# Two chained cross-attentions in f32: scores computed once and kept in SBUF, with their maxima sent round through DRAM

## The chip, the core and the metric

The kernel runs on one core of a Trainium2 chip. Its engines are named as the profile names them: PE is TensorE (matrix products), DVE is VectorE, ACT is ScalarE, POOL is GpSimd, SP is SyncE, which here issues every DMA. SBUF is the on-chip memory, PSUM the memory that TensorE writes into. The metric is device time in microseconds (us) of one execution.

## The reference

There are 4 batches, 512 queries of width C = 320, and 1024 context rows of width 512; 20 heads of 16 columns each. Two layers run one after the other, and the second takes the first one's result as its queries.

```python
# layer 0: text keys are context rows 0..1019, image ("ip") keys the last 4
q = heads(x @ W_q)
probs_t = softmax(q @ heads(text @ W_k).T * 0.25)
text_out = probs_t @ heads(text @ W_v)
qsem = l2norm(probs_t @ text)                  # 512 wide, per head and query
fused = q @ heads(ip @ W_k_ip).T * 0.25 + 0.5 * qsem @ l2norm(ip).T
ip_out = softmax(fused) * spatial_mask @ heads(ip @ W_v_ip)
x1 = (text_out + ip_out) @ W_out + b_out + x

# layer 1: text keys are context rows 0..76, ip keys the other 947
q = heads(x1 @ Wq.T)
out = softmax(q @ k_text.T * 0.25) @ v_text + softmax(q @ k_ip.T * 0.25) @ v_ip
return out @ Wo.T + bo + x1
```

The costly part is `probs_t @ text`: for each head it multiplies 512 x 1020 probabilities by a 1020 x 512 context, of which only the row norms and four inner products are needed.

## The kernel before

**Units.** A batch is cut in two halves of 256 queries (SH), a half in ten pairs of heads: 4 x 2 x 10 = 80 pair groups, counted by gi. One group has two units (class Head, one for each head). A unit multiplies exponentials of the scores by the context through a Strassen-like scheme: seven products instead of eight, each of four matmuls with 128 stationary columns, in four parts: part0 (products with context blocks 11 and 21, each also carrying value columns), part1 (t1, t2), part2 (22, t3), part3 (t4). Between them stand small sums: POOL forms s2 of two blocks of exponentials (L754), adds it to one block and subtracts it from another (L771, L774); ACT copies p and u out of PSUM (L769, L786); DVE copies p of block t1 (L782, "p5" in the code), adds c from PSUM (L762), and ACT squares and sums (L758). The products write to three PSUM banks. Value columns are loaded as narrow "windows" beside the context blocks by DMAs (L715).

**Scores, twice.** Each pair's scores are computed two times. max_fill (L437) puts 128 queries stationary and streams 512 keys; DVE takes the maximum over the keys from PSUM, negated (L663 in layer 0; L505 and L506 in layer 1). The negated maxima are transposed (pt_nm) and added to three extra rows of the queries (qa; L470 through subtract_max L462 in layer 0, L517 in layer 1). exp_fill (L448) computes the scores again with 19 rows, 16 of the head and three that carry the maxima, keys stationary and queries streaming, so that PSUM holds scores less the maximum; ACT takes the exponential directly from PSUM (L459), and for layer 0 POOL subtracts one query block from the other (L675). Each fill has one of two PSUM buffers (ps_sc).

**Order.** A list written out by hand sets it. Between the parts of a unit stand stops. stop_a (two per unit) puts a max_fill of group gi+2 and an exp_fill of group gi+1; stop_b (two per unit) takes a step of layer 1 (layer1_half L485, step L586: one max_fill of the next four heads, one exp_fill of these, and now and then the products with the values, do_pv); both also take one piece of other work from the queues: early and late (the end of a turn: softmax of the four ip scores, W_out, transposes, the queries of layer 1), proj (keys and values of the next batch). stop_c takes further steps of layer 1 near the end. The prologue computes all keys and values of batch 0. After the last group what is left of layer 1, a half batch, runs by itself. Engines take their instructions in order, and DMAs wait on SP's queue in order.

All matrix products go through one helper, mm (L74), and transposes through tr (L77), so the profile shows them under these lines; they are told apart by the tiles that they write: b (unit), mx and ex (scores), pv (layer 1's values), pt_ (others).

Of the kernel before, what the change touches and what calls it, by code (L numbers as in the profile page):

```python
# [20 lines left out]
P = 128  # L21
# [3 lines left out]
NIP = 4  # L25
# [8 lines left out]
SH = S // 2  # L34
NP = H // 2
QT = 256


R_TXT, R_IP, R_ALL, KR = 16, 17, 18, 19
# [7 lines left out]
NEVER = -1e30  # L47
ATTN_SCALE = 0.25
# [5 lines left out]
def xattn_pair(ctx_stack: ExitStack, tc: tile.TileContext, a: dict, out: bass.AP):  # L54
# [8 lines left out]
    ep = pool("ep", 8)  # L63
    st2 = pool("st2", 2)
# [13 lines left out]

    idle = [True]
# [22 lines left out]
    kq = [[cst.tile([P, T], F32, name=f"kq{l}_{i}") for i in range(1 + l)] for l in range(2)]  # L102
    qq = [[cst.tile([P, SH], F32, name=f"qq{l}_{i}") for i in range(1 + l)] for l in range(2)]
    nmz = [[cst.tile([P, 2, P], F32, name=f"nmz{l}_{i}") for i in range(1 + l)] for l in range(2)]
# [6 lines left out]
    last = cst.tile([P, 2], F32, name="last")  # L111
    wq = [cst.tile([P, NC, C], F32, name=f"wq{i}") for i in range(2)]
# [9 lines left out]
    def load_x(b, sh, pl, tag):  # L122
        t = pl.tile([P, 2, C], F32, tag=tag, name=f"{tag}_{b}_{sh}")
        nc.sync.dma_start(t, a["x"][b, sh * SH : (sh + 1) * SH, :].rearrange("(t p) c -> p t c", p=P))
        return t
# [3 lines left out]
    def load_w(b, *names):  # L129
# [11 lines left out]
        if names == ("L0_xattn_W_v",):  # L141
# [4 lines left out]

    load_chunks(wq[0], "L0_xattn_W_q")
    nc.scalar.dma_start(bo[0], a["L0_xattn_b_out"].partition_broadcast(P))


    rows0 = st3.tile([2, T], F32, tag="e1", name="rows0")
    nc.gpsimd.memset(rows0, 1.0)
    nc.gpsimd.affine_select(out=rows0[:, 0:NTXT0], in_=rows0[:, 0:NTXT0], compare_op=ALU.not_equal, fill=0.0, base=-1,
                            pattern=[[0, NTXT0]], channel_multiplier=1)

    rows = st3.tile([3, T], F32, tag="e1", name="rows")
    nc.gpsimd.memset(rows, 1.0)
    nc.gpsimd.affine_select(out=rows[:, 0:NTXT1], in_=rows[:, 0:NTXT1], compare_op=ALU.not_equal, fill=0.0, base=-1,
                            pattern=[[0, NTXT1]], channel_multiplier=1)
    nc.gpsimd.affine_select(out=rows[:, NTXT1:T], in_=rows[:, NTXT1:T], compare_op=ALU.not_equal, fill=0.0, base=0,  # L160
                            pattern=[[0, T - NTXT1]], channel_multiplier=1)
    for l in range(2):
        for i in range(1 + l):
            nc.vector.memset(qq[l][i], 0.0)
            nc.vector.memset(nmz[l][i], 0.0)
            for r in range(4):
                if l:
                    nc.scalar.dma_start(kq[l][i][32 * r + R_TXT : 32 * r + KR, :], rows)
                else:
                    nc.scalar.dma_start(kq[l][i][32 * r + R_ALL : 32 * r + KR, :], rows0[0:1, :])  # L170
                    nc.scalar.dma_start(kq[l][i][32 * r + R_IP : 32 * r + R_ALL, :], rows0[1:2, :])
                    nc.scalar.dma_start(kq[l][i][32 * r + R_TXT : 32 * r + R_IP, :], rows0[1:2, :])
    nc.vector.memset(nmz[0][0].rearrange("p j (r n) -> p (j r) n", r=4)[:, :, R_IP], NEVER)
# [3 lines left out]
                            pattern=[[0, 2]], channel_multiplier=-1)  # L177
    for n in ("21", "t4"):
        nc.gpsimd.memset(xv[n], 0.0)
# [38 lines left out]
    def transposed_half(src, name, tag):  # L218

        t = big.tile([P, NC, SH], F32, tag=tag, name=name)  # L220

        def front():
            pt = tp(f"pt_{name}_a")
            for c in range(2):
                for j in range(2):
                    tr(pt[:, c * SH + j * P : c * SH + (j + 1) * P], src[:, j, c * P : (c + 1) * P], ident)
            evac(t[:, 0:2, :].rearrange("p c s -> p (c s)"), pt)

        def back():
            pt = tp(f"pt_{name}_b")  # L230
            for j in range(2):
                tr(pt[:64, j * P : (j + 1) * P], src[:, j, 2 * P : C], ident)
            evac(t[:64, 2, :], pt[:64, 0:SH])

        return t, [front, back]

    def queries(t, w, dst, name, tag):

        o = (st2 if tag == "kst" else big).tile([P, NC, SH], F32, tag=tag, name=f"qs_{name}")

        def front():
            pt = tp(f"pt_{name}_a")
            for c in range(2):
                for i, (_, n) in enumerate(CK):
                    mm(pt[:, c * SH : (c + 1) * SH], w[:n, i, c * P : (c + 1) * P], t[:n, i, :], i == 0, i == NC - 1)
            nc.vector.tensor_scalar(o[:, 0:2, :].rearrange("p c s -> p (c s)"), pt, ATTN_SCALE, None, ALU.mult)

        def back():
            pt = tp(f"pt_{name}_b")
            for i, (_, n) in enumerate(CK):  # L250
                mm(pt[:64, 0:SH], w[:n, i, 2 * P : C], t[:n, i, :], i == 0, i == NC - 1)
            nc.vector.tensor_scalar(o[:64, 2, :], pt[:64, 0:SH], ATTN_SCALE, None, ALU.mult)
            nc.sync.dma_start(dst[0 : 2 * P, :].rearrange("(c p) s -> p c s", p=P), o[:, 0:2, :])
            nc.sync.dma_start(dst[2 * P : C, :], o[:64, 2, :])

        return [front, back]

    def projections(b):
# [5 lines left out]
        z.qd = [[dr.tile([C, SH], F32, tag=f"q{l}_{sh}", name=f"qd{l}_{b}_{sh}") for sh in range(2)] for l in range(2)]  # L264
# [4 lines left out]
        def quarter(n):  # L269
# [4 lines left out]
            def buffer(tag, shape):  # L274

                return (big if b else ep).tile(shape, F32, tag=tag if b else "e0", name=f"{tag}_{b}_{n}")
# [118 lines left out]
            if n == 0:  # L395
                v1[0:1] = [lambda: values1_first(0), lambda: values1_first(1)]
            return [[lambda: turn(0), lambda: (turn(1), sums())], [lambda: keys(0)], [lambda: keys(1)], [last_keys],
                    [lambda: values0(0), lambda: values0(1)], v1, [values_ip] if n == 3 else []]

        quarters = [quarter(n) for n in range(4)]  # L400

        for kinds in quarters if b else zip(*quarters):
            for kind in kinds:
                steps += kind
        for sh in range(2):
            hold = {}

            def first(sh=sh, hold=hold):
                t, hold["x"] = transposed_half(load_x(b, sh, big, "xin"), f"xT0_{b}_{sh}", "raw")
                hold["q"] = queries(t, wq[0], z.qd[0][sh], f"q0_{b}_{sh}", "kst")  # L410
                hold["x"][0]()

            steps += [first, lambda hold=hold: hold["x"][1](), lambda hold=hold: hold["q"][0](),
                      lambda hold=hold: hold["q"][1]()]
        return z, steps


    def pair(p):
        return p // 2, 2 * (p % 2)

    def place(l, turn, p):


        g, r0 = pair(p)
        return buffer(l, turn, g), r0

    def buffer(l, turn, g):
        return (turn * HG + g) % 2 if l else 0

    def load_pair(l, z, turn, g, i):  # L430
        k = buffer(l, turn, g)
        for r in range(2 * i, 2 * i + 2):
            c = 64 * g + 16 * r
# [580 lines left out]
```

## Time and profile before

| | us |
|---|---|
| median of 3 runs | 3852.46 (3849.34 to 3853.75) |
| profiled execution | 3851.3 |
| its span | 3849.6 |
| TensorE busy | 3710.9 (96%) |
| VectorE busy | 1622.4 (42%) |
| ScalarE busy | 1195.9 (31%) |
| GpSimd busy | 1033.4 (27%) |
| first and last unit product | 196.1, 3624.8 |

The busy times are sums over the instructions of an engine, in the one profiled execution; its span is the time from the first to the last recorded event, 1.7 us less than the time of that execution. In the views a row of the timeline has the start, the duration, the engine, the line of the code, the operation, the tile written and the tiles read, the shape, and in brackets how long the engine had idled and what released it. A row of the windows has, for a stretch of time, the busy time of PE, weight loads, DVE, ACT and POOL, then the granted clock of TensorE as a fraction of full speed, the share of the DMA engines, and GB/s.

### The profile page before, as it was taken

Reading aid. Unit: us, or ns where it says so; the run is one execution under the profiler, and the core shown is the slowest. Engines: PE = TensorE matmul, PEld = TensorE weight load, DVE = VectorE, ACT = ScalarE, POOL = GpSimd, SP = SyncE. Lnnn points to the kernel's source line nnn. Section 1 sums busy time; section 2 is a strip of 40 time slices with the busy share of each in tenths; the row PEclk is TensorE's granted clock in tenths of the full one; section 3 lists DMA queues with packets and bytes.
Section 4 is the critical chain, followed back from the end, with each engine's and each line's share of the span. In section 5 each row is a group of like instructions: output and inputs, shape, how many; then the busy total and the mean of one; then the engine's idle time right before and its main releaser. Section 6 shows DMA issues by size and latency. Waiting matters only on the chain.

```text
span 3849.6 us, 57354 instructions
## 1 busy us (share of the span) xinstructions
PE 3710.9 (96%) x21972; PEld 2633.4 (68%) x21972; DVE 1622.4 (42%) x3089; ACT 1195.9 (31%) x2424; POOL 1033.4 (27%) x1376
## 2 busy tenths in 40 slices
PE   5899999999999999999999999999999999999887
PEld 4577777677776777767776777767776676766533
DVE  1222234444434445344543545334544445355343
ACT  0122223233322333323332333323333333233222
POOL 1032233233322222223322222223332332322100
PEclk9899999999999999999999999999999999999955
DMA  6424411111232231211223232211211111111100
GB/s 178 121 67 109 108 41 17 18 28 23 59 74 64 66 89 37 53 37 28 67 52 76 62 74 48 53 34 28 61 22 31 29 22 26 30 21 25 24 19 13
DMA packets 541488, 196.11 MB, mean 51 GB/s; under 512 B 428056, under 2 KB 530936, under 8 KB 541216
## 3 DMA queue, kind: packets, MB, share of 16 engines
q1 hardware_dynamic: 540608, 192.10, 22.0%
q8 instruction: 175, 2.87, 0.3%
q14 instruction: 97, 0.79, 0.1%
q10 hardware_dynamic: 608, 0.35, 0.0%
HBM read 149.39 MB, written 40.16 MB: 49 GB/s over the span
## 4 chain that ended last, share of the span: by engine, by line
PE 91%; DVE 4%; DMA 3%; issue 1%; SPq 0%; ACT 0%; POOL 0%; POOLq 0%; DVEq 0%; ACTq 0%
PE b L74 53%; PE mx L74 11%; PE ex L74 9%; PE pv L74 5%; PE pt_k L74 4%; PE pt_v L74 4%; PE pt_y L74 2%; PE pt_q_a L74 1%; DVE den L550 1%; DVE m L506 1%; PE pt_nm L77 1%; DMA v1d<-v 1%; DMA raw<-in_ctx_dram 1%; PE pt_q_b L74 1%; DVE den L547 0%
## 5 line engine op out<-in xcount | busy, mean ns | idle before, releaser
L459 ACT ACTIVATE e<-ex 128x1024 f32<-128x1024 f32 x640 | 654.7, 1023 | 658.6 <-PE ex L74 655.6
L74 PE MATMUL ex<-qa,kq 19*128 19x256 f32 x5120 | 759.0, 417 | 10.1 <-DVE qa L517 7.3
L74 PE MATMUL mx<-kq,qq 16*128 16x512 f32 x2560 | 732.1, 673 | 28.1 <-DVE m L506 20.2
L74 PE MATMUL b<-xv_t,e 128*128 128x277 f32 x2560 | 674.2, 406 | 6.2 <-DVE c L762 6.0
L74 PE MATMUL b<-xv,e 128*128 128x277 f32 x2560 | 639.7, 402 | 0.5 <-DVE qa L470 0.5
L74 PEld LDWEIGHTS b<-xv_t,e 128*128 128x128 f32 x2560 | 471.5, 190 | 169.5 <-issue 54.0
L74 PEld LDWEIGHTS b<-xv,e 128*128 128x128 f32 x2560 | 473.8, 190 | 151.4 <-issue 44.8
L74 PEld LDWEIGHTS ex<-qa,kq 19*128 19x128 f32 x5120 | 454.9, 192 | 79.7 <-issue 16.7
L663 DVE TENSOR_REDUCE m<-mx 128x2 f32<-128x1024 f32 x320 | 390.0, 1219 | 222.5 <-PE ex L74 215.7
L758 ACT ACTIVATE junk<-c 128x256 f32<-128x256 f32 x480 | 200.2, 417 | 879.1 <-DVE c L762 879.0
L754 POOL TENSOR_TENSOR s<-e,e 128x256 f32<-128x256 f32 x320 | 228.6, 725 | 796.7 <-ACT e L459 648.3
L506 DVE TENSOR_REDUCE m<-mx 128x2 f32<-128x870 f32 (+1 forms) x320 | 364.4, 1139 | 170.1 <-PE ex L74 152.5
L675 POOL TENSOR_TENSOR e<-e 128x512 f32<-128x512 f32 x160 | 204.6, 1279 | 785.4 <-ACT e L459 776.7
L762 DVE TENSOR_TENSOR c<-b,p 128x256 f32<-128x256 f32 x320 | 134.1, 419 | 611.6 <-PE b L74 568.6
L74 PEld LDWEIGHTS mx<-kq,qq 16*128 16x128 f32 x2560 | 195.8, 191 | 246.6 <-issue 185.8
L74 PE MATMUL b<-xs,e 128*128 128x256 f32 x1280 | 318.6, 392 | 3.6 <-DVE p L782 3.6
L74 PE MATMUL b<-xs_t,e 128*128 128x256 f32 x1280 | 319.4, 392 | 1.4 <-POOL e L771 1.4
L771 POOL TENSOR_TENSOR e<-e,s 128x256 f32<-128x256 f32 x320 | 232.4, 728 | 325.9 <-PE b L74 325.9
L74 PE MATMUL b<-xs_t,s 128*128 128x256 f32 x1280 | 307.5, 383 | 0.0
L74 PEld LDWEIGHTS b<-xs,e 128*128 128x128 f32 x1280 | 233.5, 191 | 81.9 <-issue 41.6
L74 PEld LDWEIGHTS b<-xs_t,e 128*128 128x128 f32 x1280 | 229.9, 189 | 79.6 <-issue 26.2
L74 PEld LDWEIGHTS b<-xs_t,s 128*128 128x128 f32 x1280 | 241.7, 191 | 47.4 <-issue 15.6
(190 smaller groups left out, 2907.8 us busy)
## 6 DMA issues: line engine op xcount, KB each, us to landing
kq<-kd SPq DMA_DIRECT2D x320, 64.0 KB
v1q<-v1d SPq DMA_DIRECT2D x40, 373.5 KB
xv<-v0d SPq DMA_DIRECT2D x320, 42.0 KB
xv_t<-v0d SPq DMA_DIRECT2D x320, 42.0 KB
L_xattn_W_k<-in_L_xattn_W_k_dram SPq DMA_DIRECT2D x13, 640.0 KB
L_xattn_W_v<-in_L_xattn_W_v_dram SPq DMA_DIRECT2D x13, 640.0 KB
raw<-in_ctx_dram SPq DMA_DIRECT2D x32, 256.0 KB
td<-sums SPq DMA_DIRECT2D x64, 128.0 KB
```

What stands on the lines that cost most here:

```text
L74: tc.keep_in_program_order(nc.tensor.matmul(out, lhsT=lhsT, rhs=rhs, start=start, stop=stop, skip_group_check=on))
L77: tc.keep_in_program_order(nc.tensor.transpose(out, in_, ident))
L459: nc.scalar.activation(e.rearrange("p i j s -> p (i j s)"), ps.rearrange("p i n -> p (i n)"), AF.Exp)
L506: nc.vector.tensor_reduce(m[:, half, :], ps[:, :, 0 if half else NTXT1 : 512], AX.X, ALU.max, negate=True)
L550: nc.vector.reciprocal(d[:, k * SH : (k + 1) * SH], d[:, k * SH : (k + 1) * SH])
L663: nc.vector.tensor_reduce(ms[gi][:, j, half, :], ps[:, :, 0:n], AX.X, ALU.max, negate=True)
L675: nc.gpsimd.tensor_tensor(e[:, :, :, P:SH], e[:, :, :, P:SH], e[:, :, :, 0:P], ALU.subtract)
L754: nc.gpsimd.tensor_tensor(self.s2[:, 2 * k : 2 * k + 2, :], self.e("21", k), self.e("22", k), ALU.add)
L758: nc.scalar.activation(junk, x, AF.Square, accum_out=self.w["ss"][:, j, self.h, k : k + 1])
L762: nc.vector.tensor_tensor(c, x, y, ALU.add)
L771: nc.gpsimd.tensor_tensor(self.e("11", k), self.e("11", k), self.s2[:, 2 * k : 2 * k + 2, :], ALU.add)
```

## The change

Scores are computed once. A turn is now 128 queries (TURNS, 16 of them), and a group four heads of one turn: 16 x 5 = 80 groups, again of two units (class Unit, two heads each; the two row blocks of the scheme are now two heads, before they were two query tiles of one head).

fill computes half of the keys for all four heads, keys stationary, 128 queries streaming, in both ps_sc buffers; ACT copies the raw scores to SBUF (L443), and DVE takes the maximum over the four key tiles, from PSUM, for each key row and query (L444). Two fills make a group's scores. A combine joins the two halves (L617, L620; L483 in layer 1). max0 (layer 0) and do_max (layer 1) transpose these maxima (4 or 8 transposes), DVE reduces them over what were rows (L633; L495, L496), and spread (L448) transposes the result in 32 x 32 blocks (L451) and writes it to DRAM by four DMAs (L454). A DMA reads it back to all 128 partitions as bc (L637; three of them, L501 to L503, in layer 1). Then bc is added to the raw scores in SBUF, by DVE (L642, L644; L510, and half of L511 and L514) and POOL (L645; the other half of L511 and L514), and ACT takes the exponential in place (L648, L516). POOL's subtraction follows (L650).

The adds wait in a queue of their own, ew: two are taken at the end of a stop, later(1, ...) says how many stops after the maxima. The stop after part k of a group's eight parts: k = 0, 1 layer 0's fills of group gi+1; k = 3 its maxima; k = 4, 5 layer 1's fills; k = 7 layer 1's maxima; the products with layer 1's values come at k = 4 or 6, at least four stops after the maxima (wait_pv). The product with block 11 carries the value columns of both heads and is 298 columns wide, before 277; windows grow from eight DMAs per group to ten. The queries and keys of four heads are loaded by load_quad into one buffer per layer (L420); before, layer 1 had two. The last, 64-row chunk of products with K = 320 is padded with zeros to 128 rows. Layer 1's keys and values of batch 0 move from the prologue into the proj queue.

```diff
-    def max_fill(l, turn, p, c, name):
...
-            mm(ps[:, i, :], qq[l][k][r : r + D, j * P : (j + 1) * P],
-               kq[l][k][r : r + D, half * 512 : half * 512 + 512], True, True)
...
-    def exp_fill(l, turn, p, c, qa, name):
-        k, r0 = place(l, turn, p)
-        ps = ps_sc.tile([P, 2, 512], F32, tag="sc", name=f"ex{name}_{c}")
-        for j in range(2):
-            for i in range(2):
-                r = 32 * (r0 + i)
-                t = (2 * c + j) * P
-                mm(ps[:, i, j * SH : (j + 1) * SH], kq[l][k][r : r + KR, t : t + P], qa[r : r + KR, :], True, True)
-        pl = st3 if l else ep
-        e = pl.tile([P, 2, 2, SH], F32, tag=f"e{l}", name=f"e{name}_{c}")
-        nc.scalar.activation(e.rearrange("p i j s -> p (i j s)"), ps.rearrange("p i n -> p (i n)"), AF.Exp)
-    def subtract_max(l, turn, p, z, name):
...
-        lo = 32 * r0
-        qa = st2.tile([P, SH], F32, tag=f"qa{l}", name=f"qa{name}")
-        nc.vector.tensor_tensor(qa[lo : lo + 64, :], pt[lo : lo + 64, 0:SH], qq[l][k][lo : lo + 64, :], ALU.add)
...
+    def load_quad(l, z, turn, g):
+        s = TURNS[turn][1]
+        q = z.q1d[turn] if l else z.q0d[:, s * P : (s + 1) * P]
+        for r in range(4):
+            c = 64 * g + D * r
+            nc.sync.dma_start(qq[l][32 * r : 32 * r + D, :], q[c : c + D, :])
+            nc.sync.dma_start(kq[l][32 * r : 32 * r + D, :], z.kd[l][c : c + D, :])
+    def fill(l, c, m, name):
+        pl, tag = (e1p, "e1") if l and not ending[0] else (ep, "e0")
+        ps = [ps_sc.tile([P, 2, 512], F32, tag="sc", name=f"sc{name}_{c}_{i}") for i in range(2)]
+        for j in range(TH):
+            t = (TH * c + j) * P
+            for r in range(4):
+                mm(ps[r // 2][:, r % 2, j * P : (j + 1) * P], kq[l][32 * r : 32 * r + D, t : t + P],
+                   qq[l][32 * r : 32 * r + D, :], True, True)
+        lo, hi = (0, TH - c) if l == 0 else (1 - c, TH)
+        e = []
         for i in range(2):
+            e.append(pl.tile([P, 2, TH, P], F32, tag=tag, name=f"e{name}_{c}_{i}"))
+            nc.scalar.copy(e[i].rearrange("p h t s -> p (h t s)"), ps[i].rearrange("p h n -> p (h n)"))
+            nc.vector.tensor_reduce(m[:, c, 2 * i : 2 * i + 2, :],
+                                    ps[i][:, :, lo * P : hi * P].rearrange("p h (t s) -> p h s t", s=P), AX.X, ALU.max)
         return e
+    def spread(l, kinds, name):
+        zt = st2.tile([P, ZW], F32, tag="zt", name=f"zt{name}")
+        nc.vector.transpose(zt, zz[l])
+        zd = dr.tile([4 * kinds, P], F32, tag=f"z{l}", name=f"zd{name}")
+        for k in range(P // ZW):
+            nc.sync.dma_start(zd[:, ZW * k : ZW * (k + 1)], zt[ZW * k : ZW * k + 4 * kinds, :])
+        return zd
+    def later(n, steps):
+        ew.extend((stops[0] + n, f) for f in steps)
...
+        def do_fill(g, c):
+            if c and wait_pv and not ending[0]:
+                while ew:
+                    ew.popleft()[1]()
+                wait_pv.popleft()[1]()
             if c == 0:
+                ms[g] = big.tile([P, 2, 4, P], F32, tag="m1", name=f"m{name_of(g)}")
+            e1[g, c] = fill(1, c, ms[g], name_of(g))
+            if c == 0:
+                vq[g] = st2.tile([P, TT + 1, V1Q], F32, tag="v1q", name=f"v1q_{turn}_{g}")
+                nc.sync.dma_start(vq[g], z.v1d[:, :, g * 4 * V1W : g * 4 * V1W + V1Q])
+            else:
+                nc.vector.tensor_tensor(ms[g][:, 0], ms[g][:, 0], ms[g][:, 1], ALU.max)
+                if g + 1 < HG:
+                    load_quad(1, z, turn, g + 1)
+        def do_max(g):
+            m, name = ms.pop(g), name_of(g)
+            ps = ps_sc.tile([P, 4, 2, P], F32, tag="sc", name=f"mx{name}")
+            for h in range(4):
+                tr(ps[:, h, 0, :], e1[g, 0][h // 2][:, h % 2, 0, :], ident)
+                tr(ps[:, h, 1, :], m[:, 0, h, :], ident)
+            of4 = ps.rearrange("p h k t -> p h (k t)")
+            nc.vector.tensor_reduce(zz[1][:, 0:4], of4[:, :, NTXT1:], AX.X, ALU.max, negate=True)
+            nc.vector.tensor_reduce(zz[1][:, 4:8], of4[:, :, 0:NTXT1], AX.X, ALU.max, negate=True)
+            zd = spread(1, 2, name)
+            bc = big.tile([P, 2, 4, P], F32, tag="bc1", name=f"bc{name}")
+            ip, text = [zd[4 * k : 4 * k + 4, :] for k in range(2)]
+            nc.sync.dma_start(bc[:, 1], ip.partition_broadcast(P))
+            nc.sync.dma_start(bc[NTXT1:, 0], ip.partition_broadcast(P - NTXT1))
+            nc.sync.dma_start(bc[0:NTXT1, 0], text.partition_broadcast(NTXT1))
+            def do_exp(i, c):
+                e = e1[g, c][i]
+                own_bc = [bc[:, k, 2 * i : 2 * i + 2, :] for k in range(2)]
+                eng = nc.gpsimd if i else nc.vector
+                if c == 0:
+                    nc.vector.tensor_tensor(e[:, :, 0, :], e[:, :, 0, :], own_bc[0], ALU.add)
+                    eng.tensor_tensor(e[:, :, 1:, :], e[:, :, 1:, :], own_bc[1].unsqueeze(2).to_broadcast([P, 2, TH - 1, P]),
+                                      ALU.add)
+                else:
+                    eng.tensor_tensor(e, e, own_bc[1].unsqueeze(2).to_broadcast([P, 2, TH, P]), ALU.add)
+                flat = e.rearrange("p h t s -> p (h t s)")
+                nc.scalar.activation(flat, flat, AF.Exp)
+            later(1, [lambda i=i, c=c: do_exp(i, c) for c in range(2) for i in range(2)])
+            wait_pv.append((stops[0] + 4, lambda: do_pv(g)))
...
+    def fill0(gi, c):
+        if gi >= len(G):
+            return
         name = f"0_{gi}"
         if c == 0:
+            ms[gi] = big.tile([P, 2, 4, P], F32, tag="m0", name=f"m{name}")
+        e = fill(0, c, ms[gi], name)
+        for i in range(2):
+            es[gi, i, c] = e[i]
+        if c:
+            m = ms[gi]
+            nc.vector.tensor_tensor(m[:, 0], m[:, 0], m[:, 1], ALU.max)
+            for i in range(2):
+                x = m[:, 0, 2 * i : 2 * i + 2, :]
+                nc.vector.scalar_tensor_tensor(x, x, drop[:, 0:1], e[i][:, :, TH - 1, :], ALU.add, ALU.max)
+            if gi + 1 < len(G):
+                turn, g = G[gi + 1]
+                load_quad(0, zs[TURNS[turn][0]], turn, g)
+    def max0(gi):
+        if gi >= len(G):
+            return
+        turn, g = G[gi]
+        name, m = f"0_{gi}", ms.pop(gi)
+        pt = tp(f"mx{name}").rearrange("p (h t) -> p h t", h=4)
+        for h in range(4):
+            tr(pt[:, h, :], m[:, 0, h, :], ident)
+        nc.vector.tensor_reduce(zz[0][:, 0:4], pt[:, :, 0 : P - NIP], AX.X, ALU.max, negate=True)
+        nc.vector.tensor_copy(of(turn)["ips"][:, 4 * g : 4 * g + 4, :], pt[:, :, P - NIP :])
+        zd = spread(0, 1, name)
+        bc = big.tile([P, 4, P], F32, tag="bc0", name=f"bc{name}")
+        nc.sync.dma_start(bc, zd.partition_broadcast(P))
+        def do_exp(i, c):
+            e, mine = es[gi, i, c], bc[:, 2 * i : 2 * i + 2, :]
+            if c == 0:
+                nc.vector.tensor_tensor(e, e, mine.unsqueeze(2).to_broadcast([P, 2, TH, P]), ALU.add)
+            else:
+                nc.vector.scalar_tensor_tensor(e[:, :, TH - 1, :], e[:, :, TH - 1, :], drop[:, 0:1], mine, ALU.add, ALU.add)
+                nc.gpsimd.tensor_tensor(e[:, :, 0 : TH - 1, :], e[:, :, 0 : TH - 1, :],
+                                        mine.unsqueeze(2).to_broadcast([P, 2, TH - 1, P]), ALU.add)
+            flat = e.rearrange("p h t s -> p (h t s)")
+            nc.scalar.activation(flat, flat, AF.Exp)
+            if c == 0:
+                nc.gpsimd.tensor_tensor(e[:, 1], e[:, 1], e[:, 0], ALU.subtract)
+        later(1, [lambda i=i, c=c: do_exp(i, c) for i in range(2) for c in range(2)])
...
+    WINDOWS = {"11": (0, V0W + WIN), "21": (V0W, V0W + WIN), "t3": (0, WIN), "t4": (0, WIN)}
...
+            for k in {"11": (0, 1), "21": (0,)}.get(n, (1,)):
...
+    def end_stop():
+        stops[0] += 1
+        for _ in range(2):
+            if ew and ew[0][0] <= stops[0]:
+                ew.popleft()[1]()
+    def item():
+        for q in (late, proj):
+    def stop(gi, k):
+        item()
+        if k == 3:
+            max0(gi + 1)
+        if k < 2:
+            fill0(gi + 1, k)
+        if k in ((0, 1, 3, 4, 5, 7) if ending[0] else (4, 5, 7)):
+            l1_step()
+        if k in (4, 6) or ending[0]:
+            values_step()
+        end_stop()
```

## The prediction

> **What bounds the kernel now.** I read the page first (engine totals, then the chain that ended last):
>
> ```profile
> PE 3710.9 (96%) x21972; PEld 2633.4 (68%) x21972; DVE 1622.4 (42%) x3089; ACT 1195.9 (31%) x2424; POOL 1033.4 (27%) x1376
> PE 91%; DVE 4%; DMA 3%; issue 1%; SPq 0%; ACT 0%; POOL 0%; POOLq 0%; DVEq 0%; ACTq 0%
> ```
>
> TensorE is the bound and the others have half their time free. The stretches before the first semantic product (196), from there to the last one (3625), and the tail:
>
> ```profile
> 0.00:196.00 196.00, 132.45 (x504) 93.98 (x504) 35.71 (x79) 20.51 (x34) 24.42 (x64) 0.87 0.50 147
> 196.00:3625.00 3429.00, 3404.60 (x20524) 2457.31 (x20526) 1487.87 (x2851) 1126.94 (x2339) 995.46 (x1299) 1.00 0.22 48
> 3625.00:3849.60 224.60, 173.83 (x946) 82.13 (x944) 98.79 (x160) 48.50 (x53) 13.47 (x13) 0.58 0.07 19
> ```
>
> The middle holds 80 groups of two units: 3429 / 80 = 42.9 us each, and TensorE idles .3 us of that. Its clock is full; only the tail runs near half. So a group can win only what TensorE no longer does, and loses whatever it newly waits. The timeline prices a score fill:
>
> ```profile
> 1503.32 0.70 PE L74 MATMUL mx<-kq,qq 16*128 16x512 f32 x2
> 1503.33 0.70 PE L74 MATMUL ex<-qa,kq 19*128 19x256 f32 x4
> 1503.87 0.60 PE L74 MATMUL ex<-qa,kq 19*128 19x256 f32 x4
> 1504.40 1.99 PE L74 MATMUL b<-xs_t,e 128*128 128x256 f32 x8
> 1504.52 1.22 DVE L663 TENSOR_REDUCE m<-mx 128x2 f32<-128x1024 f32 x1 [0.60 <-PE ex L74]
> 1504.67 1.03 ACT L459 ACTIVATE e<-ex 128x1024 f32<-128x1024 f32 x1 [0.75 <-PE ex L74]
> ```
>
> Fill 1503.32 to 1504.40 = 1.08 us, maxima and final scores side by side, one PSUM buffer each, emptied at once by DVE (1.22) and ACT (1.03).
>
> **What the change takes from TensorE.** Eight such fills per group become four: a new fill streams 8 x 128 queries through each of four row groups, the same 1024 columns: -4.3 us. Also -.3 (pt_nm). Added: 12 transposes per group; 128-wide starts lie 109 ns apart in the trace: +1.3. 21 more value columns in one product: +.3. Keys and values of layer 1 of batch 0 leave the prologue: about 33 us over 75 groups, +.4. 42.9 - 4.3 - .3 + 1.3 + .3 + .4 = 40.3; less the .3 idle, 40 us. Prologue: 196, less 46 for the moved projections (with their waits for weights), less 23 for the old maxima and fills (173 to 196), plus 6 for two fills and their copies, 8 for the broadcast (below) and 14 for adds, exps and the first sum: 155. Tail: half the turn is left at the end (128 queries of layer 1, not 256): 25 + 5 groups x 24 + 14 = about 155 against 224.6. Both are my estimates, +-30. With no new stall: 80 x 40 + 310 = 3510.
>
> **What it adds elsewhere.** DVE: the reduces now read with a stride of 128 in PSUM (no row shows that; the unstrided 1024 row is 1.22, bounds 1 and 2 times it; I take 1, since the 160-to-40 reduce in runs of four costs what its size does). Adds: 1024 elements from SBUF about 1.3, from 640 in .825 and 256 in .425. ACT: raw copies of 1024, by the exp of that size 1.02. POOL: adds of 768 and 1024, 1.8 and 2.4, from 512 in 1.28. Per group DVE about 28, ACT 24, POOL 20 us: none is a bound by amount. SP: 1996 issues become 3916, at a mean of .43 us 1680 us: by amount no bound either.
>
> Costed at nothing: the quad loads kq (320 become 640, with qq beside them), now into single buffers. Eight issues of .43 follow a second fill, 3.4 us, and land 2.9 later; products "22", t3 and t4 of that half and the whole next half (over 15 us) cover them, and the zd writes of the maxima, next on SP, come only after t4. If that cover is gone, zd stands up to 3.4 us longer per half: inside the range. Windows (8 DMAs become 10) and v1q (40 become 80, smaller) wait on SP for TensorE, as L715 does now, and are needed a unit later. POOL's subtract L650 and sum s2 follow exps as before and are needed by the next unit, 6 us on.
>
> By order it is different. Where the built instruction streams are followed, three things stand in line:
>
> 1. *A fill takes both PSUM buffers, and is emptied one after the other*: the DVE reduce L444 waits for the ACT copy L443 of the same buffer. Copy, copy, reduce: 1.02 + 1.02 + 1.22 = 3.3 us at best, against 1.2 before.
> 2. *The maxima come back by DRAM.* After the transposes: reduces and the 32x32 transpose 1.2 to 1.7, four DMA issues 1.5, landing 1.9, the broadcast's issue .4 (it stands on SP behind windows of xv_11 and xv_21, that wait for part0 of this unit, about 3.8 after), landing 2.9: the adds cannot begin before 8.3 us. The rows used:
>
> ```profile
> 3655.53 2.12 DMA qd<-qs_q
> 3658.50 1.78 DMA qq<-qd
> ```
>
> ```profile
> 175.15 2.93 DMA raw<-in_ctx_dram
> ```
>
> The last is 256 KB, as the broadcast of bc0 (bounds 1.8 and 4.6, a load of the same kind at 19.7).
> 3. *Adds stand before reduces on DVE.* In most groups DVE's order is add L511, L514, L510, L510, then L444 twice, p5 copy; in the second half L642, L644, L444, L444, L642, L644, p5, shuffle, reciprocal (1.73). All behind the adds waits for bc: the reduces, so the second fill (it needs both buffers), and the p5 copy, so the "22" product. ACT in order: the copy u (for product t3) stands behind exps that wait for POOL's adds, and the copies L443 of the second fill behind u. The c11 sum, for product t4, stands behind reduces and the combine L617/L483.
>
> By hand, from the end of the layer-1 transposes, no DVE/POOL conflict: part0 to 3.8, fill to 4.9, products t1/t2 to 8.6; adds on DVE 8.5 to 11.7; reduces 14.1; second fill 15.2; "22" 17.0; exps to 16.9, u 17.3, t3 19.1; raw copies 19.3, reduces 20.6, combine 22.1, c11 22.6, t4 24.4, transposes 24.9: 25 us, against 15.4 for this half unstalled. Second half likewise: adds 8.3 to 10.0, reduces 12.5, fill 13.6, "22" 16.4, t3 18.3, c11 20.7, t4 22.5, eight transposes 23.4, against 18.1. Together 48.4.
>
> **DVE and POOL in each other's way.** One place shows it:
>
> ```profile
> 1282.22 1.29 POOL L675 TENSOR_TENSOR e<-e 128x512 f32<-128x512 f32 x1 [8.11 <-ACT e L459]
> 1282.48 1.32 DVE L300 TENSOR_TENSOR sums<-raw 128x256 f32<-128x256 f32 x1
> ```
>
> ```profile
> L300 DVE TENSOR_TENSOR sums<-raw x16: 424/426/1349, 6.5 to 2292.4; 128x256 f32<-128x256 f32 x16
> ```
>
> A DVE instruction with two SBUF operands, .43 alone, took 1.32 and ended .3 after POOL's. Before, nearly all DVE operations read PSUM; now both engines' adds read e and bc from SBUF and are released by the same broadcast. If they take turns, the second half ends at 27 (POOL 1.83, DVE 1.3, POOL 1.83, DVE .4 ahead of the reduces) and the first at 25.5: 52.5 us.
>
> Of the other 6.5 us of TensorE's work in a group (projections, W_out, layer 1's own) most falls into these waits; I leave 2.2 exposed, +.4 for turns ending twice as often, -.8 for groups with no layer-1 adds: 54.3. 80 x 54.3 + 310 = 4650.
>
> **Two rules against the rows.** The clock: at 720.66 TensorE stood 1.38 us beside 16-row fills and then ran
>
> ```profile
> 721.01 2.07 PE L74 MATMUL ex<-qa,kq 19*128 19x256 f32 x8 [1.38 <-DVE qa L517]
> 723.01 3.78 PE L74 MATMUL b<-xs,e 128*128 128x256 f32 x8
> ```
>
> the second taking 1.99 elsewhere; the granted clock is .50 until 727.4, so 3.4 us of work lost. The Trainium skill, "TensorE: Matmul & The Clock Gate", section "HAM oscillation — how this bites in real kernels", puts the limit at idle gaps over about 3.4 us. My timelines have one such gap in each half (8.6 to 14.1, and longer with the lock), so by the rule up to two drops a group, by the row also gaps of 1.4 to 3.4, four or more. A drop inside a stalled stretch costs less than 3.4, since what follows waits anyway. I leave it out of the sum; one exposed drop per group is +270 us. The row is nearer this kernel; hence case D.
>
> Fills of 128 columns: the row has 109 ns starts for f32 and no loss. The same page, "Back-to-back issue gap", has streams that load weights for each 128-column matmul at some 1.45 times the plain gap. By row 1.08 per fill, by rule 1.5: 320 x .4 = 130 us. I take the row; inside the stalls it would vanish largely.
>
> **The rivals.**
> - A (.50): the chain with DVE and POOL taking turns, 4650, own range 4350 to 5000. For it: the built order, the L300 rows. Against: one collision only, and of 256 elements.
> - B (.30): same chain, little conflict or shorter landings: 48.4 + 1.8 = 50.2 us, 4330 (4000 to 4450).
> - C (.12): faster. The broadcast and reduces land inside part0 to part1's cover: TensorE stays the bound with at most 2 us of stall, 3670 (3510 to 3840). It decides at (3850 - 310) / 80 = 44.2 us per group, so 4.2 us of stalls. That needs bc within about 4 us of the transposes, where my sum of shown rows is 8.3, or a DVE order in which adds do not lead. For it: 50% of DVE, ACT and POOL free.
> - D (.07): the clock at half through much of each group. Half of 40 us at half speed is +20, less 15 that the stalls absorb: +5 on A, 5050.
> - No change within .2%, about what a measurement of this kernel can tell (.01): only by chance. That the change does not do what it says is excluded: the maxima matmuls are gone from the built program.
>
> **How the numbers follow.** Most likely A: 4650. This sum stands on the profiled execution, 3851.3 us (span 3849.6, 1.7 around it), 1.2 under the median 3852.46; far below my error. Range 3950 to 5000: most of A, nearly all of B, some of D; out are C and the ends of A and D. Faster .12 (C), same .01, slower .87.
>
> **What would show it.** Right: TensorE's share at 70 to 80%, its waits naming DVE m (L444) before sc fills, ACT u before t3 and c before t4; 50 to 56 us from group to group; bc landing 8 us after the transposes; L642 or L511 on DVE well over 1.3 and 1.0 beside POOL's; sc fills 1.1; prologue and tail near 155 each. Wrong: TensorE above 90% (C); DVE adds at 1.3 beside POOL's (B); a clock under .8 in the middle (D).

## The result, and the profile after

The changed kernel takes 4836.97 us (4 runs, 4830.94 to 4844.98) against 3853.11 for the kernel before: 1.2554 times as long, with a 95% interval of 1.2527 to 1.2582. The forecast was 4650 with a range of 3950 to 5000. The profiled execution has a span of 4829.2.

The engine totals and the chain that ended last, on the page of the kernel after:

```profile
PE 3785.0 (78%) x28276; PEld 2971.5 (62%) x28276; DVE 2703.5 (56%) x3872; ACT 1803.6 (37%) x3144; POOL 1869.5 (39%) x1365
...
PE 41%; DVE 27%; DMA 16%; SPq 6%; issue 5%; ACT 4%; POOL 3%; DVEq 0%; ACTq 0%; POOLq 0%
PE b L74 30%; DMA bc<-zd 13%; DVE e L642 6%; DVE m L444 5%; DVE e L644 5%; DVE e L510 4%; PE sc L74 3%; SPq L687 2%; PE mx L77 2%; PE pt_k L74 2%; PE pt_v L74 2%; ACT e L516 2%; SPq L454 2%; DVE c L732 1%; POOL e L514 1%
```

TensorE, 91% of the chain before, is 41% of it now. DVE, the DMAs (the broadcast bc alone is 13% of the span) and SP's queue hold the rest. No engine is busy for more than 78% of the span, so none is the bound by the amount of its work.

The same three stretches as before, cut at the first product of a unit (110.8) and the end of the last (4646):

```profile
0.00:110.80 110.80, 74.88 (x353) 57.91 (x353) 29.27 (x61) 17.73 (x29) 15.61 (x46) 0.87 0.66 186
110.80:4646.00 4535.20, 3624.79 (x27007) 2849.45 (x27008) 2579.24 (x3695) 1736.31 (x3056) 1812.39 (x1292) 0.87 0.27 61
4646.00:4829.20 183.20, 85.35 (x918) 64.14 (x917) 94.97 (x117) 49.54 (x59) 41.51 (x28) 0.60 0.15 39
```

Middle: 4535.2 / 80 = 56.7 us per group, before 42.9. TensorE stands still for 910 us there (4535.2 - 3624.8), where it stood 24 before, and its granted clock fell from 1.00 to .87. Per group that is 45.3 us of TensorE's work and 11.4 of standing. From the start of one unit to that of the next, the half that carries layer 1's adds takes 29.0 us in the mean and the other 27.8.

What TensorE waits for, from the groups of the page (busy, mean ns, then the idle time ahead and what ended it):

```profile
L74 PE MATMUL sc<-qq,kq 16*128 16x128 f32 x10240 | 533.7, 323 | 484.7 <-DVE m L444 477.1
...
L74 PE MATMUL b<-xv_t,e 128*128 128x277 f32 x2560 | 744.7, 438 | 128.3 <-DVE c L732 124.4
...
L74 PE MATMUL b<-xs,e 128*128 128x256 f32 x1280 | 543.9, 599 | 248.9 <-DVE p L753 248.9
...
L645 POOL TENSOR_TENSOR e<-e,bc 128x768 f32<-128x768 f32 x160 | 382.3, 2409 | 247.6 <-DMA bc<-zd 244.9
L642 DVE TENSOR_TENSOR e<-e,bc 128x1024 f32<-128x1024 f32 x160 | 292.6, 1829 | 233.1 <-DMA bc<-zd 233.1
...
L644 DVE SCALAR_TENSOR_TENSOR e<-e,drop,bc 128x256 f32<-128x256 f32 x160 | 273.6, 1710 | 0.0
```

Three waits of the forecast are there: the second fill on the reduces, product "22" on the copy p5, t4 on the sum c. The fourth, t3 on the copy u, is hardly seen (3.6 us in all). The two adds at the head wait for bc 233 and 248 us; L642 takes 1.83 and L644, on 256 elements, 1.71.

One half in the timeline shows the chain from the start of part0 (1017.28), right behind the transposes, on. The next half starts at 1044.5:

```profile
1016.85 0.60 PE L77 MATMUL mx<-ident,m 128*128 128x128 f32 x4
...
1017.28 4.04 PE L74 MATMUL b<-xv,e 128*128 128x298 f32 x16
...
1021.26 1.17 PE L74 MATMUL sc<-qq,kq 16*128 16x128 f32 x32
...
1022.46 1.93 ACT L443 COPY e<-sc 128x1024 f32<-128x1024 f32 x2
...
1025.25 1.23 DVE L642 TENSOR_TENSOR e<-e,bc 128x1024 f32<-128x1024 f32 x1 [3.31 <-DMA bc<-zd]
1025.29 4.82 POOL L645 TENSOR_TENSOR e<-e,bc 128x768 f32<-128x768 f32 x2 [2.61 <-DMA bc<-zd]
...
1026.40 2.04 DVE L644 SCALAR_TENSOR_TENSOR e<-e,drop,bc 128x256 f32<-128x256 f32 x1
...
1028.36 1.81 DVE L444 TENSOR_REDUCE m<-sc 128x256 f32<-128x768 f32 x2
...
1029.36 0.49 PE L74 MATMUL sc<-qq,kq 16*128 16x128 f32 x4 [1.18 <-DVE m L444]
...
1030.09 2.33 DVE L642 TENSOR_TENSOR e<-e,bc 128x1024 f32<-128x1024 f32 x1
...
1030.22 1.16 PE L74 MATMUL sc<-qq,kq 16*128 16x128 f32 x28 [0.37 <-DVE m L444]
...
1032.34 1.49 DVE L644 SCALAR_TENSOR_TENSOR e<-e,drop,bc 128x256 f32<-128x256 f32 x1
...
1033.75 0.41 DVE L753 COPY p<-b 128x256 f32<-128x256 f32 x1
...
1034.31 3.75 PE L74 MATMUL b<-xs,e 128*128 128x256 f32 x8 [2.93 <-DVE p L753]
```

bc releases the adds at 1025.25, 8.0 us after the start of part0; the forecast said 8.3. The reduces start after the first two adds though ACT had copied by 1024.4, the p5 copy comes behind two more adds, only at 1033.75, and product "22" then runs at half the clock: 3.75 us where 1.99 is full.

### The profile page after: what moved, and what is told of

It reads as the page before. It is cut to its first block, busy times and chain, and to the rows that moved or that the text cites. A ratio compares the mean times of both kernels' runs of the same rounds, so it can differ in the third digit from the quotient of the medians.

```text
span 4829.2 us, 74419 instructions
## 1 busy us (share of the span) xinstructions
PE 3785.0 (78%) x28276; PEld 2971.5 (62%) x28276; DVE 2703.5 (56%) x3872; ACT 1803.6 (37%) x3144; POOL 1869.5 (39%) x1365
## 4 chain that ended last, share of the span: by engine, by line
PE 41%; DVE 27%; DMA 16%; SPq 6%; issue 5%; ACT 4%; POOL 3%; DVEq 0%; ACTq 0%; POOLq 0%
PE b L74 30%; DMA bc<-zd 13%; DVE e L642 6%; DVE m L444 5%; DVE e L644 5%; DVE e L510 4%; PE sc L74 3%; SPq L687 2%; PE mx L77 2%; PE pt_k L74 2%; PE pt_v L74 2%; ACT e L516 2%; SPq L454 2%; DVE c L732 1%; POOL e L514 1%
## 5 line engine op out<-in xcount | busy, mean ns | idle before, releaser
L74 PE MATMUL sc<-qq,kq 16*128 16x128 f32 x10240 | 533.7, 323 | 484.7 <-DVE m L444 477.1
L444 DVE TENSOR_REDUCE m<-sc 128x256 f32<-128x1024 f32 (+1 forms) x640 | 673.0, 1080 | 313.7 <-ACT e L443 313.5
L74 PEld LDWEIGHTS sc<-qq,kq 16*128 16x128 f32 x10240 | 431.9, 218 | 630.1 <-DVE m L444 546.3
L74 PE MATMUL b<-xs,e 128*128 128x256 f32 x1280 | 543.9, 599 | 248.9 <-DVE p L753 248.9
L443 ACT COPY e<-sc 128x1024 f32<-128x1024 f32 x640 | 616.4, 1015 | 202.1 <-PE sc L74 162.0
L74 PE MATMUL b<-xv,e 128*128 128x277 f32 (+1 forms) x2560 | 651.8, 407 | 11.4 <-ACT e L648 11.4
L516 ACT ACTIVATE e<-e 128x1024 f32<-128x1024 f32 x320 | 316.4, 1047 | 553.6 <-POOL e L514 387.0
L648 ACT ACTIVATE e<-e 128x1024 f32<-128x1024 f32 x320 | 337.5, 1057 | 467.0 <-DVE e L642 360.7
L645 POOL TENSOR_TENSOR e<-e,bc 128x768 f32<-128x768 f32 x160 | 382.3, 2409 | 247.6 <-DMA bc<-zd 244.9
L642 DVE TENSOR_TENSOR e<-e,bc 128x1024 f32<-128x1024 f32 x160 | 292.6, 1829 | 233.1 <-DMA bc<-zd 233.1
L511 POOL TENSOR_TENSOR e<-e,bc 128x768 f32<-128x768 f32 x80 | 203.9, 2548 | 358.5 <-DMA bc<-zd 346.4
L644 DVE SCALAR_TENSOR_TENSOR e<-e,drop,bc 128x256 f32<-128x256 f32 x160 | 273.6, 1710 | 0.0
```

Of the source, the lines that this page charges most:

```text
L74: tc.keep_in_program_order(nc.tensor.matmul(out, lhsT=lhsT, rhs=rhs, start=start, stop=stop, skip_group_check=on))
L443: nc.scalar.copy(e[i].rearrange("p h t s -> p (h t s)"), ps[i].rearrange("p h n -> p (h n)"))
L444: nc.vector.tensor_reduce(m[:, c, 2 * i : 2 * i + 2, :], ps[i][:, :, lo * P : hi * P].rearrange("p h (t s) -> p h s t", s=P), AX.X, ALU.max)
L511: eng.tensor_tensor(e[:, :, 1:, :], e[:, :, 1:, :], own_bc[1].unsqueeze(2).to_broadcast([P, 2, TH - 1, P]), ALU.add)
L516: nc.scalar.activation(flat, flat, AF.Exp)
L642: nc.vector.tensor_tensor(e, e, mine.unsqueeze(2).to_broadcast([P, 2, TH, P]), ALU.add)
```

## The experiments

The theory in three parts: (1) DVE and POOL hold each other up ("take turns") on two-operand adds from SBUF; (2) adds that wait for bc stand ahead of what TensorE needs; (3) what remains after these is again order on an in-order engine. Rivals: the way through DRAM itself, the emptying of two PSUM buffers by two engines in a row, or work that is simply there. Each kernel was timed beside the kernel before, whose median was 3847.7 to 3852.0.

**1. POOL's adds to DVE.**

```diff
-                eng = nc.gpsimd if i else nc.vector
+                eng = nc.vector
...
-                nc.gpsimd.tensor_tensor(e[:, :, 0 : TH - 1, :], e[:, :, 0 : TH - 1, :],
+                nc.vector.tensor_tensor(e[:, :, 0 : TH - 1, :], e[:, :, 0 : TH - 1, :],
```

> Edit: the adds of bc that POOL does (L645, its halves of L511 and L514) go to DVE; nothing else. Theory 1 (DVE and POOL take turns where both read two SBUF operands): DVE's adds fall back to 1.23 for 1024 elements and .47 for 256 (now 1.83 and 1.71 mean), and 768 elements cost .96 where POOL's cost 2.4 to 2.5; the adds of one half take about 5.2 us of DVE in a row instead of 6.5, exps no longer wait for POOL: 1 to 3 us less per group, 4600 to 4760. Rival (they don't hinder each other, DVE's mean comes from elsewhere): DVE has 4 us more per group at the head of its queue: 4950 to 5150.

Measured: 4548.16, ratio 1.1821 (1.1794 to 1.1848): 289 us less, though DVE has more to do. From the groups by shape:

```profile
L642 DVE TENSOR_TENSOR e<-e,bc 128x1024 f32<-128x1024 f32 x160 | 238.2, 1489 | 238.1 <-DMA bc<-zd 238.0
...
L645 DVE TENSOR_TENSOR e<-e,bc 128x768 f32<-128x768 f32 x160 | 177.6, 1110 | 0.0
...
L644 DVE SCALAR_TENSOR_TENSOR e<-e,drop,bc 128x256 f32<-128x256 f32 x160 | 103.8, 648 | 0.0
```

768 elements cost 1.11 on DVE where POOL took 2.41; L644 fell from 1.71 to .65, L642 from 1.83 to 1.49 (POOL's subtract and sums still run beside it). So the two engines do slow each other, and the move was worth somewhat more than expected (1 to 3 us per group, at least 4600; it was 3.3, from the two means of the halves). Not all of it is DVE's and POOL's time: TensorE's busy time, for the same 28276 matmuls, fell with its waits from 3785.0 to 3699.3. What waits for bc is as before: 238 us.

**2. Adds behind both fills' reduces and the combine.** Each add but POOL's L645 got a fixed place in the program's order, and all got two stops more. The second delay, in max0, is changed in the same way (not shown).

```diff
-            later(1, [lambda i=i, c=c: do_exp(i, c) for c in range(2) for i in range(2)])
+            later(3, [lambda i=i, c=c: do_exp(i, c) for c in range(2) for i in range(2)])
...
-                nc.vector.tensor_tensor(e, e, mine.unsqueeze(2).to_broadcast([P, 2, TH, P]), ALU.add)
+                tc.keep_in_program_order(nc.vector.tensor_tensor(e, e, mine.unsqueeze(2).to_broadcast([P, 2, TH, P]), ALU.add))
```

> Edit: the adds are taken two stops later and held behind what DVE has before them in the program's order, so that the four reduces L444 and the combine of a half stand ahead of them; who does which add is unchanged. Theory 2 (the wait for bc at the head of DVE's queue is the price): second fills start right after part1, c11 is the only sum still behind adds: 45 us per group, 3800 to 4100. Rival (the maxima's way through DRAM itself is the price, wherever the adds stand): exps come late, the wait moves to the values' products and to part0, 4500 or more.

Measured: 4315.8, 1.1213 (1.1181 to 1.1244): 521 us less, but 216 above the top of what the theory gave, and under the rival's 4500. The fills' wait for L444 fell from 477 to 66 us and that of product "22" for p5 from 249 to 2. But the sum c, as the expectation had it, still stood behind adds, and t4's wait for it grew from 124 to 454 us:

```profile
L74 PE MATMUL b<-xv_t,e 128*128 128x277 f32 x2560 | 803.0, 464 | 540.3 <-DVE c L732 454.5
```

**3. The same, one stop later: adds behind the c sums.** (`later(4, ...)`, and the products with layer 1's values at least five stops after the maxima; the last two groups keep the old delays.)

> Edit: as the run with the adds behind the fills, one stop later still: adds stand behind the c sums and, for the second two, behind the reduces of the next maxima; the values' products wait one stop longer. Theory 2: no add is ahead of anything TensorE waits for soon; TensorE's own 40 us per group and 1 to 3 us of waits (t4 on c11, part0 on the exps): 3550 to 3750, below the kernel before. Rival as there: the exps, now a stop later, hold part0 and the values' products: 4000 or more.

Measured: 4050.69, 1.0522 (1.0498 to 1.0546). With POOL's adds left on POOL, 786 us of the loss are gone by order. In the new places the adds also meet less: POOL's L645 takes 1.83 in the mean, not 2.41. The time was 300 us above the theory's band, though, and inside the rival's (4000 or more), but without the waits that the rival named: part0 waits 11 us for exps, as before, and the values' products 15. The timeline shows what was left: now ACT's order was wrong.

```profile
2634.98 1.06 ACT L516 ACTIVATE e<-e 128x1024 f32<-128x1024 f32 x1 [5.32 <-POOL e L514]
2635.94 0.35 ACT L756 COPY u<-b 128x256 f32<-128x256 f32 x1
...
2636.35 2.13 PE L74 MATMUL b<-xv_t,e 128*128 128x277 f32 x8 [1.97 <-ACT u L756]
...
2641.35 3.68 PE L74 MATMUL b<-xv_t,e 128*128 128x277 f32 x8 [2.87 <-DVE c L732]
```

An exp waits 5.3 us for POOL, the copy u stands behind it, then the raw copies, the reduces, c11; and after the second wait TensorE runs at about half its clock (3.68 for 2.13; granted .54 from 2641.5 to 2645).

**4. No way through DRAM.** bc is zeros made once (the maxima are not subtracted); the adds are fixed in the program's order ahead of the second fill, a second edit beside the first. Layer 1's three DMAs go in the same way (not shown).

```diff
-        bc = big.tile([P, 4, P], F32, tag="bc0", name=f"bc{name}")
-        nc.sync.dma_start(bc, zd.partition_broadcast(P))
+        bc = bcz[:, 0]
```

> Edit: bc is a tile of zeros made once, so the maxima are computed, transposed and written to DRAM, but not read back (the exponentials are taken without subtracting the maxima); the adds are held in program order, first ones right behind the 32x32 transpose, so adds still stand ahead of the second fill. Theory 2: without the 8 us the adds run in part0's time: reduces at 8 to 9 us of a half, 42 to 44 us per group, 3650 to 3900. Rival (copy, copy, reduce, reduce, and DVE and POOL taking turns, set the pace): 4300 or more.

Measured: 4028.03, 1.0468 (1.0447 to 1.0489): 809 us less, between the two expectations. What is left stands at the fills (168 us) and the sum c (204); p5 costs 17. So most of the loss can be taken away from either end: by having bc at once, or by leaving it 8 us late and moving what waits for it (run 3, within 23 us of this one).

**5. The exps in program order on ACT,** on top of run 3:

```diff
-            nc.scalar.activation(flat, flat, AF.Exp)
+            tc.keep_in_program_order(nc.scalar.activation(flat, flat, AF.Exp))
```

> Edit: on top of the run with the adds behind the c sums (4051), the exps are held in program order on ACT, so that the copy u and the raw copies of a half don't stand behind an exp that waits for POOL's add. Theory 3 (what is left there is ACT's order: in its trace TensorE waited 70 us for u and 218 us for c, and the clock halves after the longer ones): 100 to 250 us less, 3800 to 3950. Rival (the exps are merely late and something else then waits for them): values' products or part0 wait, 4000 to 4100.

Measured: 3818.77, .9924 (.9908 to .9940): 232 us less, as the theory expected, and below the kernel before. TensorE's wait for u is gone (70 us) and that for c fell from 218 to 142.

**6. The combine behind the c sums,** on top of run 5: the join L617, L620 (L483) is put in a queue that is taken after part2, not at once.

> Edit: as the last, and the join of the two halves of the maxima (L617 and L620, L483) stands behind the c sums on DVE instead of between them. Theory 3: c11 comes 1.5 us earlier in the first half, .7 in the second, so t4 hardly waits: 60 to 150 us less than the last, 3700 to 3850, under the kernel before. Rival (TensorE's own work of 3400 us with the waits for projections and the end of each turn is what is left): within 40 us of the last.

Measured: 3797.61, .9866 (.9844 to .9887): 21 us less, which is the rival's band (within 40), not the theory's. The page's totals, the whole middle (80 groups), and four groups in a row from the second of a turn on, without projections of keys and values:

```profile
PE 3403.7 (90%) x28276; PEld 2710.4 (71%) x28276; DVE 2362.1 (62%) x3872; ACT 1804.2 (48%) x3144; POOL 1685.0 (44%) x1365
...
107.80:3636.00 3528.20, 3250.70 (x27090) 2593.16 (x27092) 2257.55 (x3725) 1744.85 (x3069) 1638.49 (x1296) 0.97 0.35 79
...
2843.45:2992.93 149.48, 144.04 (x1322) 115.00 (x1321) 103.17 (x166) 84.12 (x147) 80.65 (x59) 1.00 0.31 64
```

The four take 37.4 us per group, 36.0 of it TensorE's work, clock 1.00. Four such groups of the kernel before (794.72 to 948.44) take 38.4, with 38.1 of work: the saved fills, less the new transposes, show as 2.1 us of work and 1.0 of time, though run 6's four hold a little of a turn's end as well. The whole kernel gains less, because the first group of each turn takes about 52 us, not 37, and groups with projections 43 to 60. Over the span TensorE's busy time fell from 3710.9 to 3403.7, but its idle time grew from 139 to 390.

**7. The evacuation alone: reduces from SBUF,** on the changed kernel:

```diff
-                                    ps[i][:, :, lo * P : hi * P].rearrange("p h (t s) -> p h s t", s=P), AX.X, ALU.max)
+                                    e[i][:, :, lo:hi, :].rearrange("p h t s -> p h s t"), AX.X, ALU.max)
```

> Edit: the changed kernel with one thing else: the reduces L444 read ACT's copies in SBUF instead of PSUM, so that a second fill waits for ACT alone. Theory 2 (DVE's queue behind bc is the price): second fills go early, but the copy p5 and the sum c11 still stand behind adds and reduces, so the wait moves from the fills to product 22 and t4: 4550 to 4830. Rival (emptying both PSUM buffers by two engines in a row is the price): 4300 or less.

Measured: 4865.06, 1.2633 (1.2615 to 1.2652): no gain, 28 us more than the changed kernel, 35 above the theory's band and far from the rival's. The groups show the wait moving:

```profile
L74 PE MATMUL b<-xs,e 128*128 128x256 f32 x1280 | 543.4, 599 | 793.9 <-DVE p L753 787.7
...
L74 PE MATMUL sc<-qq,kq 16*128 16x128 f32 x10240 | 396.6, 288 | 31.1 <-ACT e L443 24.5
```

The fills' wait fell from 485 to 31 us and product "22" waits 794 instead of 249 (sums 734 and 825), for the same DVE queue. The PSUM buffers were the first to be late, not the main cause. The edit isn't clean, though: the reduce of 1024 elements over four key tiles took 1.91 from SBUF in the mean, from PSUM 1.21, and DVE was busy for 197 us more in all, which may hide a gain of up to about that size.

**8. The turn's end in three pieces,** on top of run 6: norms, square root and fused scores, softmax at three stops, each with a fixed place.

```diff
-        late.extend([lambda: None] * 2 + [turn_ip, add_ip, turn_out, multiply])
+        late.extend([lambda: None, norms, fused, softmax, turn_ip, add_ip, turn_out, multiply])
```

> Edit: on top of the run with the join behind the sums (3798), the end of a turn (norms, softmax of the ip scores) is taken in three pieces at three stops, each held behind what DVE and ACT have before it. In that run's trace groups take 37 us, but the first of each turn 52: the second half of the reduces waits for a raw copy that stands on ACT behind the square root of the norms. Theory 3 (order on in-order engines is the price, here too): 5 to 10 us less in each of 15 turns: 3650 to 3725. Rival (the first group of a turn has that much work of its own): 3770 to 3830.

Measured: 3786.68, .9832 (.9815 to .9848): the fastest of all, but only 11 us less, in the rival's band and not the theory's, and the interval touches that of run 6. First groups of a turn did fall from 52 to 47; second ones rose from 38 to 39, and a new wait took part of the gain:

```profile
L77 PE MATMUL pt_p<-ident,pe 128*80 128x128 f32 x16 | 5.9, 368 | 56.0 <-DVE pe L825 56.0
```

**9. As run 8, with one empty stop more ahead of that transpose.**

> Edit: the run with the turn's end in pieces (3787), with one empty stop more between the softmax of the ip scores and its transpose, for which TensorE waited 56 us in all there. Theory 3: that wait goes, with the half clock behind it: 40 to 80 us less, 3705 to 3745. Rival (the next thing of the queue is then late by as much): within 20 us of 3787.

Measured: 3895.1, 1.0111 (1.0093 to 1.0130): 108 us slower. The first groups fell to 42, but the second ones rose from 39 to 50:

```profile
L74 PE MATMUL sc<-qq,kq 16*128 16x128 f32 x10240 | 442.2, 296 | 124.3 <-DMA qq<-q1d 62.8
```

Layer 1's queries for the new turn are made at the end of the same queue; moved by a stop, their load missed the fill. The rival named this kind and not its size.

**10. As run 8, with all adds on DVE.** Layer 0's add that moves is fixed in the program's order here, which it was not in run 1.

> Edit: as the last, and all adds of bc on DVE (as in the first run of this kind, there 289 us faster). Theory 1 with 2: the taking of turns cost so much there because the adds stood ahead of what TensorE waits for; here they don't, so little is won: within 60 us of the last either way; the small instructions of the turn's end fall from 1 to 2 us to about .25. Rival (taking turns costs the same everywhere): another 200 us or more less.

Measured: 4003.31, 1.0392 (1.0375 to 1.0408): 217 us slower, where almost the same edit had won 289. Neither expectation held. The fills' wait for the reduces rose from 53 to 142 us, that of the transpose of run 8 from 56 to 83, and TensorE's busy time, for as many matmuls, from 3426.5 to 3544.7: its work got slower by 118 us. A likely reason is that with the adds out of the way POOL's share ran in time that nobody waited for, and on DVE it stands ahead of other work; that was not tested.

**11. As run 8, with bc as zeros.**

> Edit: the run with the turn's end in pieces (3787), with bc a tile of zeros made once, so that the maxima are written to DRAM but not read back or subtracted; the order of all adds is unchanged. In the changed kernel the same edit won 809 us. Theory 2 (the way through DRAM costs only where adds stand ahead of what TensorE waits for): within 40 us of 3787. Rival (the way itself costs, order or not): 200 us or more less.

Measured: 3816.64, .9918 (.9902 to .9935). The edit that won 809 us in the changed kernel wins nothing here: 30 us more, within the 40 that the theory allowed. TensorE stands still as long as in run 8 (354 and 359 us) and only takes longer for its work (3462 and 3427), so the 8 us through DRAM cost only where something that TensorE needs stands behind them.

## Why the prediction was right

- *bc by 8.3 us after the transposes*: 8.0 in the half shown. The sum of shown rows held.
- *What stands behind it*: L444, p5, u and c were named, and L444 (477 us), p5 (249) and c (124) are TensorE's largest waits; u is not among them. Runs 2, 3, 5 and 11 show that their place in the queues is the price; run 7 that the two PSUM buffers by themselves are not the main one.
- *The sum came close partly by luck.* The forecast's group of 54.3 us was 40 of TensorE's work and 14.3 of standing still. Measured were 45.3 and 11.4, together 56.7: less stall than forecast and slower work, two errors of opposite sign.
- *Halves of 25.5 and 27*: 29.0 and 27.8, which hold other work too. The half shown ends 27.2 us after its start, as summed, but not in the forecast's way. With DVE and POOL in each other's way its reduces were to end at about 16 (8.3, the adds of both engines, 2.5 of reduces; 12.5 without); they end at 12.9. What came instead is the second pair of DVE's adds ahead of p5, 2.33 and 1.49 us long (1.21 and .47 at their fastest), and half-clock products.
- *DVE and POOL* were reckoned one-sidedly: I let POOL keep its time and delayed DVE alone. Both lose: L645 took 2.41 (1.80 at its fastest) and DVE's L644 1.71 (.47 at its fastest). Run 1 won 289 us by moving POOL's adds, net of what they cost DVE; the prediction's step for taking turns was (52.5 - 48.4) x 80 = 330.
- *The clock was left out of the sum*, with one exposed drop per group at +270. It belonged in: TensorE's busy time is 3785.0 us, and 3403.7 in run 6 for the same 28276 matmuls, 381 us or 4.8 per group more. How much of that fell into time that was lost anyway was not separated. In the half shown the granted clock is .50 from 1034.4 to 1037.8, in the half before it from 1008.1 to 1011.5; both are on the chain. The Trainium skill's limit of idle gaps over about 3.4 us ("TensorE: Matmul & The Clock Gate", "HAM oscillation — how this bites in real kernels") covers the second, which follows a wait of 6.05, but not the first: gaps of 1.18, .37 and 2.93 within 6.1 us stand before it. In run 3 it was 1.97 and 2.87 within 7. As at the row of 1.38, shorter gaps were enough; where the limit lies was not measured.
- *Fills*: 1.17 us in one piece at full clock, not 1.08; the 1.5 that would follow from that page's 1.45 times ("Back-to-back issue gap") is not seen there. The mean of all 320, with those cut in two and those at half clock, is 1.67 (533.7 / 320).
- *Reduces with a stride, at the unstrided 1.22*: 1.21 from PSUM. *Quad loads, costed at nothing*: fills wait 6 us in all for them. *Prologue and tail* of 155 each: 110.8 and 183.2, 44 less and 28 more; together 16 us.
- *TensorE's 40 us per group without stalls*: 3250.7 / 80 = 40.6 in the middle of run 6, at a mean clock of .97. The 3510 of no new stall at all was not reached in any run.
- *Rival C* (44.2 us per group decides) named a DVE order in which the adds do not lead. That is what the runs after it made, and run 6, with 3528.2 / 80 = 44.1, is faster than the kernel before. *Rival B*'s sign, DVE's adds at 1.3 beside POOL's, is not seen (L642 1.83). *Rival D* did not come: .87 in the middle.

## What to carry to other kernels

When scores are kept and a correction returns by a long way, place everything that waits for it behind what the bounding engine needs next, on every in-order engine, and hold it there: fixing the exps' place on ACT won 232 us by itself (run 5). Count a stall of the bounding engine for more than its length where its clock follows its waits: from the changed kernel to run 6 TensorE's idle time fell by 654 us (1044 to 390) and its busy time for the same matmuls by another 381. Ask of a shared buffer or a slow engine what else stands in the same queue before blaming it: moving the reduces to SBUF moved the wait to another product. Moving work between engines has no fixed sign: almost the same move won 289 us with the adds in the way and lost 217 with them out of it.

## What the runs showed of the hardware that was not expected

Two-operand SBUF adds on POOL were slowed as well as DVE's when they ran together (768 elements: 1.80 to 2.88 us in the kernel after, 1.83 in the mean in run 3, where they seldom meet). In run 6, twenty-element instructions of the turn's end on DVE took up to 2.26 us beside a POOL add, and .11 to .28 with no POOL instruction beside them. A reduce over four tiles that stand 128 elements apart took 1.91 us from SBUF and 1.21 from PSUM, at times when no POOL instruction ran as well; over three tiles (768 elements) the shortest took 1.01 and .94. TensorE's clock halved after waits of 2.9 us in the two stretches shown, each with a shorter wait a few us ahead of it.
